# Four fused layers on one core: frequency gate's product and sum on GpSimd, layer 0's MLP finished ahead of layer 3, an order of its own for the last image's MLP rounds

## Chip, cores and metric

The kernel runs on one core of one Trainium2 chip. The metric is the device time of one execution in microseconds, the median of several executions. A core has five engines that run beside each other, each in its own program order: TensorE (PE, matmuls; its weight loads are listed as PEld), VectorE (DVE), ScalarE (ACT), GpSimd (POOL) and SyncE (SP, which here only issues DMAs). An engine that waits for a semaphore holds everything behind it in its order.

## What is computed

Four images of 192 channels and 64 x 64 pixels go through four layers; all is fp32. Layer 0 is a transformer block with a deformable 3x3 convolution for the queries, channel attention and an MLP. Layer 1 is a non-local block (4096 x 4096 scores an image). Layer 2 is attention in overlapping windows, followed by a projection, a frequency gate and a gated MLP. Layer 3 is a masked 3x3 depthwise convolution whose weights depend on the image's mean. What the change touches, cut from the reference:

```python
# layer 0, end
h1 = layer_norm(xs2, gamma2, beta2)
xs3 = xs2 + gelu(h1 @ w_fc1 + b_fc1) @ w_fc2 + b_fc2
# layer 2, after the windows
def _hft(x, w, b):
    a = 3.0 * x
    for s in (2, 4, 8):
        a = a - upsample(mean_pool(x, s), s)
    return sigmoid(dwconv3(a, w, b)) * x
x1 = x + _hft(conv1x1(out, proj_w, proj_b), hft_w, hft_b)
z = gelu(conv1x1(ln_c(x1), fc1_w, fc1_b))
z1, z2 = split(z, 2, axis=1)                      # 384 channels each
z = z1 * dwconv3(ln_c(z2, sgn_g, sgn_b), sg_w, sg_b)
return x1 + conv1x1(z, fc2_w, fc2_b)
```

A layer norm here needs 1 / sqrt(variance + eps). In parts of the kernel it is Sqrt on ACT and a reciprocal on DVE, in others Ln and Exp (with the factor -0.5) on ACT alone.

## The kernel before

The images are handled one after the other, with work of the next image woven in. For each image b:

1. `keys` (L910): the non-local block's keys and values from layer 0's result, which `mlp0` has written to DRAM in eight chunks. For b = 1 and 2, `offsets(b + 1)` (eight layer norms and the deformable convolution's offsets for the image after) goes chunk by chunk with it.
2. `layer1`: scores (L963) and their product with the values (L1031); the deformable convolution's gather for image b + 1 is woven in.
3. `windows`: layer 2's attention.
4. `rest(b)`: `project`, `mlp`, `layer3`. For images 0 to 2, the steps of `mlp0(b + 1)`, layer 0's attention result and MLP for the next image, are woven in: each part of `rest` yields a credit, and each whole credit takes one step of `mlp0`. What is left of `mlp0` when `layer3` has been issued is drained at the end (`for _ in other`). The last image (`alone`) has nothing to weave in; there some of the depthwise taps run as matmuls with diagonal weights on PE (`HFT_PE`, `GATE_PE`).

`project` handles six units of 128 x 1024. `first(u)` projects (L1475), builds the pools and the filtered image (L1482 to L1513). `second(u)` does the nine depthwise taps (helper lines L1370, L1373 and L1377, on DVE; `gt`, `ht` and L1368 are taps on PE), the sigmoid (L1523, ACT), the product with the projected image (L1525) and the sum into `x` (L1526). `ahead()` starts the layer norm of the MLP's first pair of chunks. The order of instructions on the engines is Tile's scheduler's there; roots are Sqrt (L362) and reciprocal (L364), because the list `in_order` is empty.

`mlp` has four rounds j, one for each pair of chunks, in an order written out by hand (`tc.manual_schedule`): `widen` (L1574, L1576, GELU L1580) of six blocks of 128 hidden channels; the gate's layer norm (`gate_mean` L1586, `gate_difference` L1590, `gate_square` L1595, `gate_variances`, `gate_scale` L1613 and L1617); the depthwise taps of the pair before (`upper_taps`, five of them; `lower_taps` four more one round later, ending in L1647, which makes `z1`); `narrow` (L1659 and L1664) of the pair two rounds back; `end` (L1673) adds into `x`. In it the roots are Ln and Exp, and `table()` loads the ACT table that comes next, once.

`layer3` takes the mean, makes the weights (L1771 to L1789), then for six units ACT starts (L1819), DVE adds three taps (L1838), and a DMA stores the unit (L1840, L1844).

The lines that set the handover, in `rest`:

```python
yield from project(b, x, others, oi.pop(), psums, HFT_PE if alone else (), ahead)
yield from mlp(b, x, sums, sb, psums, GATE_PE if alone else (), hn)
yield from layer3(b, x, sums, psums, alone)
...
for part in main():
    credit += part
    while credit >= 1.0:
        next(other, None)
        credit -= 1.0
for _ in other:
    pass
```

`NCH` is 8, the number of chunks of 512 pixels; `mlp0` has 33 steps.

Of the kernel before, what the change touches and what calls it, by code (L numbers as in the profile page):

```python
# [13 lines left out]
ALU = mybir.AluOpType  # L14
# [19 lines left out]
LN_EXP, GELU = "natural_log_exp_and_others", "gelu"  # L34
# [47 lines left out]
def conv_seq_kernel(ctx: ExitStack, tc: tile.TileContext, a, out: bass.AP):  # L82
# [1340 lines left out]
    def project(b, x, others, oi, ps, taps, ahead):  # L1423
# [3 lines left out]
        with ExitStack() as s:  # L1427
# [88 lines left out]
            def second(u):  # L1516
# [25 lines left out]
    def mlp(b, x, sums, sb, ps, taps, hn):  # L1542


        with ExitStack() as s:
# [134 lines left out]
            with tc.manual_schedule():  # L1680
                in_order.append(None)
                for j in range(pairs):
                    lo, hi, upper, lower = 2 * j, 2 * j + 1, j - 1, j - 2
                    if lower >= 0:
# [11 lines left out]
                    if upper >= 0:  # L1696
                        upper_taps(upper, 0, 2)
                    end()
                    widen(j, (5, 0))
                    gate_mean(lo)  # L1700
                    gate_mean(hi)
                    if upper >= 0:
                        upper_taps(upper, 0)
                        upper_taps(upper, 1, 2)
                    gate_difference(lo)
                    gate_square(lo)
                    gate_difference(hi)
                    widen(j, (1,))
                    gate_square(hi)
                    widen(j, (2,))  # L1710
                    if upper >= 0:
                        upper_taps(upper, 1)
                        upper_taps(upper, 2, 2)
                    gate_variances(lo, hi)
                    norm = None
                    if j + 1 < pairs:
# [3 lines left out]
                    if norm is not None:  # L1720
# [5 lines left out]
                    if norm is not None:  # L1726
# [3 lines left out]
                for m in range(3):  # L1730
                    lower_taps(pairs - 2, m)
                    yield 1.0
                narrow(pairs - 2, (0, 1, 2))
# [314 lines left out]
```

## Time and profile before

| what | us |
|---|---|
| median of 3 runs | 6800.64 (6798.39 to 6806.05) |
| profiled execution | 6757.88 |
| its span | 6756.1 |
| PE busy | 6155.1 |
| DVE busy | 4694.1 |
| ACT busy | 3599.2 |
| POOL busy | 2065.4 |
| projection of image 0 | 1866 to 1999 |
| its MLP | 1999 to 2303 |
| layer 3 and the handover to image 1 | 2303 to 2336 |
| keys and layer norms of image 1 | 2336 to 2456 |
| layer 1 of image 1 begins | 2456 |
| projection of the last image | 6339 to 6443 |
| its MLP | 6437 to 6722 |
| its layer 3 | 6722 to 6756 |

The profile shows one execution. Busy shares over the whole span mix stages with different limits, so the prediction reads them by stage. Lines of a group name an instruction's source line, engine, operation, and output and input tiles by the program's names. After "idle" stands the time in which the engine did nothing before such an instruction, and what ended it.

### The profile page before, as it was taken

The numbers are of one execution on the slowest core, as the hardware profiler recorded it, in microseconds if no ns is written. First come the engines' busy times: TensorE is split into PE (matmuls) and PEld (weight loads), VectorE is DVE, ScalarE is ACT, GpSimd is POOL, SyncE is SP. The second block draws the span as 40 slices with busy tenths as digits, with TensorE's granted clock in tenths as the row PEclk, the third lists the DMA queues.
The fourth block names the chain that finished last, engine by engine and source line by source line (L and its number), as shares of the span: only waits on it lengthen the run. The fifth ranks groups of instructions, "written<-read, shape, count | busy, mean of one in ns | idle before, by whom it ended". The sixth has DMA issues, their size and how long they took to land.

```text
span 6756.1 us, 115795 instructions
## 1 busy us (share of the span) xinstructions
PE 6155.1 (91%) x45392; PEld 4180.0 (62%) x45392; DVE 4694.1 (69%) x6908; ACT 3599.2 (53%) x6136; POOL 2065.4 (31%) x2276
## 2 busy tenths in 40 slices
PE   7687999999989899999998899999998889999986
PEld 4455578786644458887654457878664457776532
DVE  3664279985677758996576848988567867765656
ACT  3664368774444358885444338877444435544332
POOL 2654057662200027672210007765220000012200
PEclk8788999999989899999999999999999999999998
DMA  6885156661010156663110047665101010010000
GB/s 188 260 280 177 54 177 217 215 196 42 8 43 15 59 181 200 219 211 93 29 31 26 17 132 218 216 208 165 35 24 30 17 54 10 15 28 22 4 7 21
DMA packets 330496, 699.37 MB, mean 104 GB/s; under 512 B 60077, under 2 KB 217181, under 8 KB 329182
## 3 DMA queue, kind: packets, MB, share of 16 engines
q0 software_dynamic: 92736, 455.22, 21.0%
q1 hardware_dynamic: 236382, 235.95, 12.3%
q8 instruction: 358, 5.87, 0.4%
q14 instruction: 188, 1.54, 0.1%
q10 hardware_dynamic: 832, 0.79, 0.0%
HBM read 611.25 MB, written 78.87 MB: 102 GB/s over the span
## 4 chain that ended last, share of the span: by engine, by line
PE 51%; DVE 17%; ACT 4%; issue 4%; DMA 2%; SPq 0%; POOL 0%; another core or an unknown queue 0%; DVEq 0%; ACTq 0%; POOLq 0%
PE y L1031 8%; PE s L963 7%; PE h L634 3%; PE v L1196 2%; PE h L1574 2%; DVE ha L1377 2%; PE qk L1121 2%; PE qk L1122 2%; PE t L1204 1%; DVE gate L1377 1%; PE zm L1586 1%; DVE ga L1377 1%; PE h L1576 1%; PE s L1157 1%; PE rb L1270 1%
## 5 line engine op out<-in xcount | busy, mean ns | idle before, releaser
L616 POOL DMA_INDIRECT ring<-table,idx x1152 | 1634.7, 1419 | 1132.5 <-issue 217.8
L963 PE MATMUL s<-ths,ph 96*128 96x256 f32 x4096 | 991.5, 383 | 8.5 <-ACT xo L626 2.7
L963 PEld LDWEIGHTS s<-ths,ph 96*128 96x128 f32 x4096 | 784.0, 193 | 137.1 <-ACT ths L957 4.7
L622 ACT ACTIVATE row<-ring,pos 128x384 f32<-128x384 f32 x1152 | 672.0, 608 | 204.3 <-DVE xo L627 111.3
L1031 PE MATMUL y<-sc,gx 128*97 128x256 f32 x3008 | 724.7, 383 | 18.4 <-ACT yn L1037 15.1
L623 DVE SCALAR_TENSOR_TENSOR row<-ring,fr,row 128x384 f32<-128x384 f32 x1152 | 674.8, 613 | 91.6 <-ACT row L622 63.1
L1031 PEld LDWEIGHTS y<-sc,gx 128*97 128x97 f32 x3008 | 492.5, 165 | 150.8 <-ACT yn L1037 16.5
L626 ACT ACTIVATE xo<-row,pos 128x192 f32<-128x192 f32 x1152 | 485.8, 448 | 156.9 <-remote 63.8
L627 DVE SCALAR_TENSOR_TENSOR xo<-row,fr,xo 128x192 f32<-128x192 f32 x1152 | 447.1, 412 | 123.3 <-issue 60.6
L1028 DVE TENSOR_TENSOR sc<-sc,mbs 128x1024 f32<-128x1024 f32 x376 | 453.4, 1218 | 46.1 <-ACT mbs L989 26.5
L965 ACT COPY sc<-s 128x1024 f32<-128x1024 f32 x376 | 377.5, 1004 | 177.5 <-PE s L963 141.5
L970 DVE TENSOR_TENSOR top<-top,sc 128x1024 f32<-128x1024 f32 x282 | 344.5, 1222 | 137.4 <-ACT sc L965 115.9
L634 PE MATMUL h<-ti,xo 128*128 128x192 f32 x2304 | 437.1, 328 | 0.0
L1029 ACT ACTIVATE sc<-sc 128x1024 f32<-128x1024 f32 x376 | 393.4, 1053 | 75.6 <-DVE sc L1028 66.5
L634 PEld LDWEIGHTS h<-ti,xo 128*128 128x128 f32 x2304 | 390.9, 190 | 29.0 <-issue 8.6
L1180 DVE TENSOR_REDUCE es<-ex 128x6 f32<-128x384 f32 x264 | 133.3, 546 | 365.0 <-ACT ex L1176 365.0
L634 PE MATMUL h<-kept,xo 128*128 128x192 f32 x960 | 255.9, 402 | 114.1 <-DVE xo L627 61.5
L634 PEld LDWEIGHTS h<-kept,xo 128*128 128x128 f32 x960 | 183.0, 224 | 209.5 <-DVE xo L627 98.6
L1624 POOL COPY gate<-gate 128x192 f32<-128x192 f32 x12 | 4.2, 351 | 1000.4 <-ACT gate L1617 855.0
L1377 DVE SCALAR_TENSOR_TENSOR ga<-gate,v,ga 128x1024 f32<-128x1024 f32 x234 | 300.4, 1284 | 6.7
L1031 PE MATMUL y<-se,gx 128*97 128x256 f32 x1088 | 268.3, 387 | 8.6 <-ACT se L1029 8.1
L858 ACT ACTIVATE gl<-h,bias_fc 128x256 f32<-128x256 f32 x384 | 151.2, 474 | 232.9 <-PE h L851 232.5
(391 smaller groups left out, 11213.0 us busy)
## 6 DMA issues: line engine op xcount, KB each, us to landing
ti<-table SPq DMA_DIRECT2D x768, 48.0 KB
ring<-table,idx POOLq DMA_INDIRECT x1152
xnd<-xn SPq DMA_DIRECT2D x4, 3270.0 KB
xi<-in_x_dram SPq DMA_DIRECT2D x32, 384.0 KB
xk<-xd SPq DMA_DIRECT2D x32, 384.0 KB
xd<-xc SPq DMA_DIRECT2D x64, 192.0 KB
table<-tt SPq DMA_DIRECT2D x32, 384.0 KB
xc<-xd SPq DMA_DIRECT2D x60, 192.0 KB
```

The costliest lines, as they stand in the source:

```text
L616: nc.gpsimd.indirect_dma_start(out=gt.rearrange("p q r c -> p (q r c)"), out_offset=None, in_=corners, in_offset=bass.IndirectOffsetOnAxis ...
L622: nc.scalar.activation(row, gt[:, 0], AF.Copy, scale=pos[:, t, 9 + tap : 10 + tap])
L623: nc.vector.scalar_tensor_tensor(row, gt[:, 1], fr[:, t, 9 + tap : 10 + tap], row, ALU.mult, ALU.add)
L626: nc.scalar.activation(xo[:, j, :], row[:, 0, :], AF.Copy, scale=pos[:, t, tap : tap + 1])
L627: nc.vector.scalar_tensor_tensor(xo[:, j, :], row[:, 1, :], fr[:, t, tap : tap + 1], xo[:, j, :], ALU.mult, ALU.add)
L634: nc.tensor.matmul(acc[m // 2][:, bass.ts(m % 2, C)], lhsT=xo.rearrange("p j c -> p (j c)")[:, bass.ts(m, 128)], rhs=tt, start=t == 0 and ...
L963: nc.tensor.matmul(p[:, t, :], lhsT=ph[:, bass.ts(G * g + t, 128)], rhs=ths[i], start=True, stop=True)
L965: nc.scalar.copy(to, p)
L1028: nc.vector.tensor_tensor(ex, ex, mbs[i].unsqueeze(1).to_broadcast([128, G, QN]), ALU.add)
L1029: nc.scalar.activation(ex, ex, AF.Exp)
L1031: nc.tensor.matmul(py, lhsT=gx[:, G * g + t, :], rhs=ex[:, t, :], start=g == 0 and t == 0, stop=g == NG - 1 and t == G - 1,)
L1377: nc.vector.scalar_tensor_tensor(acc[:, b], src(tap, b), w[:, tap : tap + 1], acc[:, b], ALU.mult, ALU.add)
```

## The change

Four things are changed.

- In `project`, product and sum of the frequency gate go from VectorE to GpSimd. `project` runs with ACT's instructions in program order and `in_order` active, so that its layer norms, and those of `mlp0` that are woven in there, take their roots by Ln and Exp, and tables are loaded ahead by `table()`.
- In `mlp` for images 0 to 2, `narrow(lower, (0, 1))` and `narrow(lower, (2,))` become one `narrow(lower, (0, 1, 2))`; the tail's credits go from 0.5, 0.6 and 0.7 to 0.9 each; after `mlp` a credit of 32 lets all of `mlp0` be issued ahead of `layer3`.
- In `mlp` for the last image the round has an order of its own: the narrow comes after the second widen, means and differences; the upper taps stand later, two of the three in the norm's steps; the tail puts upper taps of the last pair between lower taps of the one before, and narrows block by block.
- The output DMAs of `layer3` go from SP's queue to GpSimd's for images 0 to 2.

The diff, cut to its core:

```diff
-            if name == GELU:
-                nc.scalar.preload_act_table(AF.Gelu)
+            if name in (GELU, SIGMOID):
+                nc.scalar.preload_act_table(name)
...
+                table(SIGMOID)
                 nc.scalar.activation(acc, acc, AF.Sigmoid, bias=VW["l2_hftb"][:, k])
                 cols = bass.ts(u, UN)
-                nc.vector.tensor_tensor(acc, acc, prs.pop(u), ALU.mult)
-                nc.vector.tensor_tensor(x[:, cols], x[:, cols], acc, ALU.add)
+                nc.gpsimd.tensor_mul(acc, acc, prs.pop(u))
+                nc.gpsimd.tensor_add(x[:, cols], x[:, cols], acc)
...
                     if lower >= 0:
                         lower_taps(lower, 2)
-                        narrow(lower, (0, 1))
-                        narrow(lower, (2,))
...
+                    if taps:
+                        widen(j, (5, 0))
+                        gate_mean(lo)
+                        gate_mean(hi)
+                        gate_difference(lo)
+                        gate_square(lo)
+                        gate_difference(hi)
+                        if lower >= 0:
+                            narrow(lower, (0, 1, 2))
+                        end()
+                        widen(j, (1,))
+                        gate_square(hi)
+                        if upper >= 0:
+                            upper_taps(upper, 0, 2)
+                        widen(j, (2,))
+                        gate_variances(lo, hi)
+                        if upper >= 0:
+                            upper_taps(upper, 0)
+                            upper_taps(upper, 1, 2)
+                    else:
+                        if lower >= 0:
+                            narrow(lower, (0, 1, 2))
...
                     yield 1.0
-                    if norm is not None:
+                    if taps and upper >= 0:
+                        upper_taps(upper, 1)
+                        upper_taps(upper, 2, 2)
+                    if more:
                         links(norm, VARIANCE)
...
+                one, two = pairs - 2, pairs - 1
+                if taps:
+                    lower_taps(one, 0)
+                    upper_taps(two, 0)
+                    lower_taps(one, 1)
+                    upper_taps(two, 1)
+                    narrow(one, (0,))
+                    lower_taps(one, 2)
+                    narrow(one, (1,))
+                    narrow(one, (2,))
+                    upper_taps(two, 2)
                     end()
-                    yield 0.5
-                    upper_taps(pairs - 1, m)
-                    yield 0.6
-                    lower_taps(pairs - 1, m)
-                    yield 0.7
-                narrow(pairs - 1, (0, 1))
-                narrow(pairs - 1, (2,))
+                    for m in range(3):
+                        lower_taps(two, m)
+                        narrow(two, (m,))
+                else:
...
+                        yield 0.9
...
+            by = nc.sync if alone else nc.gpsimd
...
-                    nc.sync.dma_start(out=flat[0:M, bass.ts(u, UN)], in_=o)
+                    by.dma_start(out=flat[0:M, bass.ts(u, UN)], in_=o)
...
-                yield from project(b, x, others, oi.pop(), psums, HFT_PE if alone else (), ahead)
+                with tc.manual_schedule(engines={mybir.EngineType.Activation}):
+                    in_order.append(None)
+                    yield from project(b, x, others, oi.pop(), psums, HFT_PE if alone else (), ahead)
+                    in_order.pop()
                 yield from mlp(b, x, sums, sb, psums, GATE_PE if alone else (), hn)
+                yield 4.0 * NCH
                 yield from layer3(b, x, sums, psums, alone)
```

More of the change, by code (lines that the diff above doesn't have):

```diff
@@ L33 @@
 NEG = -1.0e30
-LN_EXP, GELU = "natural_log_exp_and_others", "gelu"
+LN_EXP, GELU, SIGMOID = "natural_log_exp_and_others", AF.Gelu, AF.Sigmoid
 WP = 66
@@ L1683, in mlp @@
                     lo, hi, upper, lower = 2 * j, 2 * j + 1, j - 1, j - 2
+                    more = j + 1 < pairs
                     if lower >= 0:
@@ L1693, in mlp @@
                         lower_taps(lower, 2)
-                        narrow(lower, (0, 1))
-                        narrow(lower, (2,))
[L1696 to L1714, printed above, removed]
+                    if taps:
[20 more added lines that the diff above has]
+                            narrow(lower, (0, 1, 2))
+                        if upper >= 0:
+                            upper_taps(upper, 0, 2)
+                        end()
+                        widen(j, (5, 0))
+                        gate_mean(lo)
+                        gate_mean(hi)
+                        if upper >= 0:
+                            upper_taps(upper, 0)
+                            upper_taps(upper, 1, 2)
+                        gate_difference(lo)
+                        gate_square(lo)
+                        gate_difference(hi)
+                        widen(j, (1,))
+                        gate_square(hi)
+                        widen(j, (2,))
+                        if upper >= 0:
+                            upper_taps(upper, 1)
+                            upper_taps(upper, 2, 2)
+                        gate_variances(lo, hi)
@@ L1715, in mlp @@
                     norm = None
-                    if j + 1 < pairs:
+                    if more:
                         norm = pair_norm_steps(x, j + 1, sb, ps, f"l2n2_{b}_{j + 1}")
@@ L1719, in mlp @@
                     yield 1.0
-                    if norm is not None:
+                    if taps and upper >= 0:
+                        upper_taps(upper, 1)
+                        upper_taps(upper, 2, 2)
+                    if more:
                         links(norm, VARIANCE)
@@ L1725, in mlp @@
                     hns.pop(j)
-                    if norm is not None:
+                    if more:
                         hns[j + 1] = links(norm)
@@ L1729, in mlp @@
                         upper_taps(upper, 2)
[L1730 to L1733, printed above, removed]
-                for m in range(3):
-                    upper_taps(pairs - 1, m, 2)
-                    end()
-                    yield 0.5
-                    upper_taps(pairs - 1, m)
-                    yield 0.6
-                    lower_taps(pairs - 1, m)
-                    yield 0.7
-                narrow(pairs - 1, (0, 1))
-                narrow(pairs - 1, (2,))
+                one, two = pairs - 2, pairs - 1
[9 more added lines that the diff above has]
+                    upper_taps(two, 2)
+                    end()
+                    for m in range(3):
+                        lower_taps(two, m)
+                        narrow(two, (m,))
+                else:
+                    for m in range(3):
+                        lower_taps(one, m)
+                        yield 1.0
+                    narrow(one, (0, 1, 2))
+                    for m in range(3):
+                        upper_taps(two, m, 2)
+                        end()
+                        yield 0.9
+                        upper_taps(two, m)
+                        yield 0.9
+                        lower_taps(two, m)
+                        yield 0.9
+                    narrow(two, (0, 1))
+                    narrow(two, (2,))
                 end()
@@ L1843, in layer3 @@
                     for h in range(2):
-                        nc.sync.dma_start(out=to[:, :, h], in_=o[half(h)].rearrange("p (k n) -> p k n", k=2))
+                        by.dma_start(out=to[:, :, h], in_=o[half(h)].rearrange("p (k n) -> p k n", k=2))
                 yield 0.7
```

## The prediction

> **What bounds the kernel now.** I read the page's first part, then a table of stretches by stage, then the waits of TensorE (PE) inside the stretches that the change touches, then single instructions in the timeline. From the page:
>
> ```profile
> PE 6155.1 (91%) x45392; PEld 4180.0 (62%) x45392; DVE 4694.1 (69%) x6908; ACT 3599.2 (53%) x6136; POOL 2065.4 (31%) x2276
> ```
>
> PE is busy for 91% of the span, so most microseconds can only come out of PE's 600 us of idle time. The table of stretches says where it idles (columns: stretch, its length, busy us and instructions of PE, weight loads, VectorE (DVE), ScalarE (ACT), GpSimd (POOL), then granted clock, DMA share, GB/s):
>
> ```profile
> 1866.00:1999.00 133.00, 109.62 (x441) 57.50 (x440) 123.25 (x203) 55.88 (x74) 4.40 (x12) 0.87 0.16 43
> 3460.00:3591.00 131.00, 104.29 (x438) 55.08 (x437) 123.20 (x203) 55.90 (x75) 4.40 (x12) 0.90 0.15 42
> ...
> 6339.00:6443.00 104.00, 93.13 (x234) 39.11 (x234) 75.25 (x132) 26.91 (x29) 9.75 (x26) 0.91 0.05 13
> 6481.00:6531.00 50.00, 45.08 (x181) 20.70 (x181) 23.95 (x25) 20.04 (x29) 0.37 (x2) 0.93 0.00 0
> 6531.00:6600.00 69.00, 56.17 (x206) 23.93 (x206) 45.13 (x47) 20.54 (x29) 0.91 (x3) 0.90 0.00 0
> 6600.00:6656.00 56.00, 46.87 (x172) 18.80 (x170) 38.91 (x38) 14.65 (x22) 0.00 (x0) 0.97 0.00 0
> 6656.00:6722.00 66.00, 46.74 (x112) 18.14 (x112) 45.57 (x52) 6.03 (x8) 1.26 (x5) 0.87 0.02 4
> ...
> 2336.00:2456.00 120.00, 115.66 (x936) 60.96 (x935) 34.39 (x46) 40.34 (x75) 0.00 (x0) 0.93 0.48 140
> ```
>
> The first two are the projection of images 0 and 1 (image 2: 132 us, the same shares): DVE is busy 93% and PE 80 to 82%, so DVE sets the pace. The third is the last image's projection, where PE leads (90%) and DVE is at 72%. The next four are rounds 1, 2, 3 and the tail of the last image's MLP: PE idles 4.9, 12.8, 9.1 and 19.3 us, with nothing woven in. The last row is the way into layer 1 of image 1: PE is full. What PE waits for, in the projection of image 0 (columns: us in total, times, longest):
>
> ```profile
> PE pb_l0m L382 <- DVE r_l0m L364: 7.4, 2, 4.5
> ...
> PE pb_l2n L1418 <- DVE r_l2n L364: 4.5, 1, 4.5
> ```
>
> in round 2 of the last image, and in its tail:
>
> ```profile
> PE f L1659 <- DVE z L1647: 7.8, 3, 5.1
> ```
>
> ```profile
> PE f L1659 <- DVE z L1647: 18.4, 4, 12.9
> ```
>
> So two places can give time: a DVE-bound projection in which PE also waits 11.9 us for reciprocals queued on DVE, and a last MLP whose narrow matmuls stand in PE's order before work that was ready.
>
> **Part 1, the projection of images 0 to 2.** DVE loses six products (L1525, 1219 ns) and six sums (L1526, 1207 ns): 14.6 us an image; and four reciprocals (L364: 3 x 947 ns and 1753 ns), which Ln and Exp on ACT replace: 4.6 us. Together 19.2 of 123. ACT's table loads grow from 15 to 18 (1283 ns each, +3.8 us) in an engine busy 56 of 133; I take that as hidden behind DVE.
>
> GpSimd gets twelve 128x1024 operations with two inputs. The trace has none; the nearest row is L1244, 128 elements with two inputs, 0.45 us when alone. Copies give the fixed part: 528 elements 640 ns, 16 elements 195 ns, so 0.87 ns an element above 0.18 us. Lower end (two inputs at a copy's rate) 1.1 us; upper end (eight times 0.45) 3.6 us; my value (0.45 - 0.18)/128 = 2.1 ns an element, 2.3 us. Twelve take 27 us (13 to 43) of an engine that is busy 4.4 of 133. Nobody reads the sum for tens of microseconds but the pair norm, which takes units 0 and 4, two units earlier; the latency of about 6 us is covered.
>
> What is not free is the memory behind it. Two pairs in the timeline (columns: start, us, engine, line) show DVE and POOL in each other's way:
>
> ```profile
> 1681.17 0.96 DVE L1171 TENSOR_TENSOR ex<-ex,mx 128x768 f32<-128x768 f32 x1
> ...
> 1681.35 1.50 POOL L1244 TENSOR_TENSOR ot<-ot,ot 102x128 f32<-102x128 f32 x2 [15.53 <-ACT ot L1238]
> ```
>
> ```profile
> 1609.66 1.23 DVE L1171 TENSOR_TENSOR ex<-ex,mx 128x768 f32<-128x768 f32 x1
> ```
>
> The two POOL operations take 1.50 us instead of 0.90: the first ends only after the DVE operation that began before it. And the same DVE operation takes 1.23 instead of 0.96 us when a POOL copy (1609.45 to 1610.09) began first. In the projection the taps L1377, with both inputs in SBUF, are 62 of the 104 us that DVE keeps, nearly back to back. If DVE stands still for none of POOL's 27 us, it is left with 104 us and PE (110) leads; if for all of them, it has 131. My value is the taps' share, 60%: 16 us, DVE 120, 3 us less than now. For PE's waits behind reciprocals I add 2 us. **Value -5 an image, -15 in all; bounds -12 (PE's waits and its 110 us stay) and +8 (27 - 19) an image.**
>
> [...]
>
> **Part 2, the last image's projection.** DVE has room; -2 (bounds -6 and +4, by the 2.5 us that PE waits for the reciprocal and by a sum that comes late).
>
> **Part 3, rounds of images 0 to 2.** PE's order becomes 12 of L1659, then 12 of L1664. Before, 8 of L1664 (1.94 us) ran while the third z was awaited; now they stand behind that wait (0.7 us long as it was). Two rounds an image: 6 x 1.9 = +11 at most, 0 if woven work waits elsewhere anyway; value +9.
>
> **Part 4, the last image's MLP.** Round 2: after the first widen (5.7 us) PE now has widen (5.6) and means (5.4) before the narrow, so it needs z at +17, +19 and +21 us of the round; DVE's z are ready at 10.7, 15.9 and 21.1. The 7.8 us wait goes. Taps of 3.7 us each stand in the norm's chain (4.2 us waiting for the square). ACT is late next: z1 needs the buffer that the narrow reads, so its squares begin at +27, but the variances stand behind widen and taps at +36. The round ends near 57.5 instead of 68.7: -11. Round 1: only the norm's wait is filled: -3. Round 3 saves 6 to the gates' scaling. Tail: DVE no longer sits from 6678.7 to 6694 behind 60 tap matmuls (26 us); these now run in thirds of 8.7 us beside lower taps of 5.2. The last third stands behind the third narrow, so DVE waits about 10 us there. DVE's chain gives an end 10 us earlier for round 3 and tail together. **Value -24; bounds -32 and -12.**
>
> **Part 5, handover.** Layer 0's last chunk is computed before the last narrow; layer 3 comes after both. Now:
>
> ```profile
> 2325.55 8.01 PE L737 MATMUL o<-bias,ident 128*128 128x384 f32 x24 [1.36 <-DVE xa L874]
> 2335.82 1.68 PE L910 MATMUL tp<-xk,phiT 96*96 96x512 f32 x3 [2.26 <-DMA xk<-xd]
> ```
>
> The keys start some 18 us earlier (2318). But layer 3's 25 us of DVE begin near 2325 instead of 2308, and the keys' evictions stand between them in DVE's order; the fifth waits for PSUM freed near 2351. The next loads stand behind that one on SP's queue, so the third layer norm, before at 2351.7, starts near 2362. Eight norms then run one after another (76 us before), but PE is free of keys meanwhile, so the 25 us of offsets behind the last norm shrink to about 19: +3 (bounds -4 and +10), twice. From image 2 to 3 there are no norms: -3.5 (bounds -8 and +3). Output DMAs of images 0 to 2 move from SP to POOL's queue; POOL is idle there, nobody reads them.
>
> **Sum.** -15 - 2 + 9 - 24 + 6 - 3.5 = -29.5. The profiled execution has 6757.9 us (span 6756.1 and 1.8 around it), 43 us under the median 6800.64; the difference carried to the median gives **6771**.
>
> **Rivals.**
> - GpSimd is beside, not in the way: projection -12 each, in all -50, 6750. For it: L1377 beside POOL memsets keeps its 743 ns. Against: those only write.
> - GpSimd holds DVE up (the other side): operations of 3.6 us, DVE still for all 43 us, +24 an image; -14.5 + 72 = +57, 6858. It makes the kernel slower from 9.4 us an image on, that is with over 28.6 us of DVE blocked.
> - Handover: norms, not PE, set the way into layer 1, +20 each (18 us of layer 3 and 2 of queue) in place of +3: in all +4.5, 6805.
> - The last image's order gives 5 instead of 24, because DVE's taps are the chain: -10.5, 6790.
>
> **Chances.** Forecast 0.50, GpSimd free 0.15, GpSimd in the way 0.15, handover 0.12, last order 0.08. A measurement of this kernel tells 0.2% (13.6 us) from no change. Faster: 0.47 of the forecast and 0.15, 0.62; same: 0.03 + 0.09 of the handover + 0.08, 0.20; slower: 0.15 + 0.03, 0.18. Range 6742 to 6816: it leaves out most of the second rival (0.13) and the far ends of the others (0.05), and takes in the handover and the last order; the forecast's own range is 6755 to 6787.
>
> **What would show it.** The projection's stretch: 128 us, its L1526 on POOL at 2.3 us (over 3 speaks for the second rival), L1377's mean above 1275 ns or DVE idle behind POOL. Round 2 of the last image: no wait of L1660 on DVE, 57 us between its widens. The tail from the last gate to layer 3: 56 us. First L910 after image 0's MLP some 18 us earlier against the MLP's start, the first score matmul of layer 1 within 10 us. Wrong above all if DVE's taps lengthen by more than 20 us an image.

## The result and the profile after

The changed kernel takes **6901.47 us** (median of 4 runs, 6872.33 to 6915.78) against 6803.35 for the kernel before on the same chip (6798.39 to 6807.80): a ratio of 1.0145, with a 95% interval of 1.0115 to 1.0175. It is slower by 98 us; the forecast was 6771, faster by 30. The profiled execution has 6872.33 us, its span 6870.6. The experiments ran on other chips, where the kernel before takes 6622 to 6627 us and the changed kernel is slower by a ratio of 1.0123 (1.0098 to 1.0149); so ratios are compared, or times of one chip. Lines of the changed kernel stand one or two above those of before (L1525 is L1526, L1659 is L1660, L1647 is L1648).

The line of the page that opened the prediction, now:

```profile
PE 6229.8 (91%) x45392; PEld 4225.4 (62%) x45392; DVE 4687.1 (68%) x6847; ACT 3604.0 (52%) x6153; POOL 2182.2 (32%) x2348
```

PE runs the same 45,392 matmuls and is busy 75 us longer with them, and the mean granted clock went from 0.952 to 0.941: this is the first hint. The table of stretches (columns as in the prediction: stretch, length, busy us and count of PE, weight loads, DVE, ACT, POOL, then granted clock, DMA share, GB/s), for the projection of image 0, the last image's projection and its round 2, and the keys of image 1:

```profile
1886.00:2013.90 127.90, 102.94 (x418) 53.90 (x417) 114.29 (x180) 57.15 (x77) 35.03 (x22) 0.88 0.14 40
6464.00:6572.00 108.00, 88.79 (x216) 37.18 (x217) 69.33 (x115) 25.63 (x29) 32.92 (x36) 0.86 0.05 13
```

```profile
6665.30:6721.60 56.30, 51.63 (x205) 22.34 (x204) 45.13 (x46) 20.65 (x30) 0.64 (x2) 0.98 0.00 1
```

```profile
2352.00:2504.50 152.50, 137.05 (x964) 72.62 (x962) 57.65 (x84) 45.49 (x80) 8.76 (x22) 0.79 0.44 130
```

Three readings. In the projection DVE is busy 114 of 128 us although 14.6 us of products and sums and 4.6 of reciprocals are gone from it. The stretch that the prediction took for this stage, 1866 to 1999, ends 7.5 us inside the MLP; up to the MLP's first matmul the kernel before has

```profile
1866.70:1991.50 124.80, 102.25 (x420) 54.34 (x419) 116.56 (x196) 54.73 (x73) 4.40 (x12) 0.87 0.16 44
```

so DVE is busy 2 us less than before, and the stage is 4 us longer (128.7 us from its first matmul to the MLP's, against 124.8). Round 2 of the last image takes 56.3 us instead of 68.7. The keys of image 1 take 152.5 us instead of 120, at a granted clock of 0.79 instead of 0.93.

Put stage by stage (from the first instruction of a stage to that of the next), with the changed kernel's second profile, that of the control below, beside a kernel whose projections, MLPs and keys of images 0 to 2 are those of before (`e2_last_order`), both on the experiments' chips; in us, images 0, 1, 2:

| stage | unchanged | changed | difference |
|---|---|---|---|
| projection | 123.7, 123.3, 124.8 | 129.5, 129.0, 129.0 | +15.7 |
| MLP, to the next image's first key | 343.0, 343.2, 343.6 | 337.8, 338.5, 341.0 | -12.5 |
| keys, to layer 1 | 120.1, 119.7, 27.9 | 153.3, 153.1, 54.9 | +93.6 |
| last projection | 98.1 | 107.9 | +9.8 |
| last MLP and layer 3 (unchanged: profile of before) | 319.4 | 298.5 | -20.9 |

The sum is +85.7; the medians of the changed kernel's chip differ by 80.0 (6704.93 and 6624.93). Stretches that the change does not touch differ by 3 to 10 us between these two profiles (29 in all, not in the table), so a few us in one stage say little. Nearly all of the loss is the keys at the three handovers; GpSimd's part, the two rows of projections, is a quarter of that, and the last image's order gives what was forecast.

**What the keys do.** PE's timeline of the changed kernel where the keys of image 1 begin (columns: start, us, engine, line, operation, tiles, shapes, count, and in brackets the idle time ahead and what ended it):

```profile
2351.38 1.96 PE L910 MATMUL tp<-xk,phiT 96*96 96x512 f32 x4
...
2356.23 0.25 PE L1812 MATMUL pt<-mean,w1T 128*48 128x1 f32 x2
...
2357.44 1.05 PE L1823 MATMUL pw<-t,w2T 48*128 48x1 f32 x8
2358.42 0.88 PE L1826 MATMUL pw<-t,w2T 48*64 48x1 f32 x16
2359.23 2.17 PE L915 MATMUL g<-gT,xk 96*128 96x96 f32 x16
2361.20 3.62 PE L910 MATMUL tp<-xk,phiT 96*96 96x512 f32 x4
2364.61 3.57 PE L915 MATMUL g<-gT,xk 96*128 96x96 f32 x16
...
2392.62 3.73 PE L910 MATMUL tp<-xk,phiT 96*96 96x512 f32 x4 [1.84 <-DVE gx L918]
```

Four L910 take 1.96 us at the start and 3.62 from 2361 on: half clock. The granted clock is 0.5 for 58.0 us here, for 58.0 and 54.6 at the other two handovers. The kernel before has this too, but for 17.1 us at the first two and not at all at the third. Its timeline at image 2:

```profile
3926.27 2.38 PE L910 MATMUL tp<-xk,phiT 96*96 96x512 f32 x4 [2.10 <-DMA xk<-xd]
...
3931.80 3.62 PE L910 MATMUL tp<-xk,phiT 96*96 96x512 f32 x4
3935.22 3.57 PE L915 MATMUL g<-gT,xk 96*128 96x96 f32 x16
3938.58 3.62 PE L910 MATMUL tp<-xk,phiT 96*96 96x512 f32 x4
3941.99 3.25 PE L394 MATMUL pm_l<-xi,mean 96*96 96x512 f32 x4
3945.08 1.92 PE L915 MATMUL g<-gT,xk 96*128 96x96 f32 x16
3946.84 1.88 PE L910 MATMUL tp<-xk,phiT 96*96 96x512 f32 x4
```

PE is busy for 50.6 us of each of the three longer stretches and for all of the 17.1, and at a granted clock of 0.5 half of that is taken as lost (four L910 lose 1.66 of 3.62 us), so the clock alone costs (50.6 - 17.1) / 2 = 17 us, again 17, and 25 at image 3: 59 of the 93.6, as an estimate.

The traces also show behind what the half clock ended. In all sixteen of them the granted clock changes only on a grid of 3.41 us; a step is one such stretch. In the fence above it came back after the step from 3941.33 to 3944.74, the first that held nothing but matmuls of 512 columns: the end of a key's L910 and, directly behind it, L394 of the first layer norm. Of 356 steps at half clock in all traces with only L910, L915 and L394 in them, 334 were filled to less than 98% by L910 and L394, and the clock came back behind two of these; it came back behind 20 of the other 22 (in the traces before and after alone, behind none of 52 and all of 3). In the kernel before a layer norm stands behind the third L910, and there the half clock ends; in the changed kernel all norms stand behind all keys, and between them L915 with its 96 columns comes after every L910. This is read off the traces; no experiment varied it alone.

The last line of the changed kernel's fence shows the other part of the loss: a key waits for the eviction (L918) of an earlier one. DVE's timeline of the changed kernel shows where evictions stand:

```profile
2388.21 3.63 DVE L1880 SCALAR_TENSOR_TENSOR out<-x,w,out 128x448 f32<-128x448 f32 x6 [2.47 <-issue]
...
2392.02 0.55 DVE L918 COPY gx<-g 128x384 f32<-128x384 f32 x1
...
2406.53 0.56 DVE L918 COPY gx<-g 128x384 f32<-128x384 f32 x1 [6.22 <-PE g L915]
2409.94 1.22 DVE L398 TENSOR_TENSOR d_l<-xi,pm_l 96x1024 f32<-96x1024 f32 x1 [2.85 <-PE pm_l L394]
```

They stand between layer 3's taps (L1880), and the first layer norm (L398) of the image after comes behind all eight keys, 58.6 us after the first key; before, norms and keys alternated from +19.0 us on. The last of the eight norms is 119.6 us behind the first key instead of 82.6.

### The profile page after: what moved, and what is told of

Read it like the earlier page. It is cut to its first block, busy times and chain, and to the rows that moved or that the text cites. A ratio compares the mean times of both kernels' runs of the same rounds, so it can differ in the third digit from the quotient of the medians.

```text
span 6870.6 us, 115882 instructions
## 1 busy us (share of the span) xinstructions
PE 6229.8 (91%) x45392; PEld 4225.4 (62%) x45392; DVE 4687.1 (68%) x6847; ACT 3604.0 (52%) x6153; POOL 2182.2 (32%) x2348
## 5 line engine op out<-in xcount | busy, mean ns | idle before, releaser
L1377 DVE SCALAR_TENSOR_TENSOR ga<-gate,v,ga 128x1024 f32<-128x1024 f32 x234 | 300.3, 1283 | 6.5
L858 ACT ACTIVATE gl<-h,bias_fc 128x256 f32<-128x256 f32 x384 | 150.7, 474 | 237.2 <-PE h L851 236.7
```

Source lines behind the costliest of these rows:

```text
L1377: nc.vector.scalar_tensor_tensor(acc[:, b], src(tap, b), w[:, tap : tap + 1], acc[:, b], ALU.mult, ALU.add)
```

## The experiments

**1. Undo the handover** (changed kernel; everything else kept):

```diff
-                        yield 0.9
+                        yield 0.5          # and 0.6, 0.7
...
-            by = nc.sync if alone else nc.gpsimd
+            by = nc.sync
...
-                yield 4.0 * NCH
```

> The changed kernel with the handover alone undone: no credit of 32, the tail's credits 0.5, 0.6 and 0.7 again, layer 3's output DMAs on SP's queue. Theory A (the loss is in the handover: the keys of the next image run among layer 3's instructions, their evictions wait on VectorE, and the granted clock falls to 0.5): the three stretches from projection to layer 1 lose their 26 to 31 us each, so 6901 - 85 = about 6815, ratio to before about 1.002. Theory B (GpSimd's product and sum hold VectorE up, in the projection and wherever else): hardly a change, 6890 or more. Theory C (a lower clock over the whole run): no change.

Measured: 6650.86 us, ratio 1.0051 (1.0032 to 1.0071). The keys are back at 112.2, 119.4 and 27.9 us, projections stay at 127 to 129, the last MLP at 298.6. The keys of image 1 kept the clock and took 112.2 us, those of image 2 lost it for 17 us and took 119.4. Of the changed kernel's 1.2% some 0.7% go with the handover.

**2. The last image's order alone** (kernel before, with the new order of rounds and tail for the last image only).

```diff
+                    if taps:
+                        widen(j, (5, 0))
...
+                    else:
+                        if lower >= 0:
+                            narrow(lower, (0, 1))
+                            narrow(lower, (2,))
```

> The kernel before with the last image's order of rounds alone. The trace of after has this MLP at 262 us instead of 284, so theory A and B both expect 6803 - 22 = 6781, ratio 0.997; if the gain comes only from what the projection before it leaves over, it is below 10 us.

Measured: 6596.00 us, ratio 0.9968 (0.9947 to 0.9988). In the profile the last MLP takes 291.9 us instead of 319.4, a gain of 27.5; the medians show 21 to 26 (the interval reaches from 8 to 35). This part is right, in kind and in size.

**3. Product and sum back on DVE** (changed kernel, order of ACT and the roots by Ln and Exp kept):

```diff
-                nc.gpsimd.tensor_mul(acc, acc, prs.pop(u))
-                nc.gpsimd.tensor_add(x[:, cols], x[:, cols], acc)
+                nc.vector.tensor_tensor(acc, acc, prs.pop(u), ALU.mult)
+                nc.vector.tensor_tensor(x[:, cols], x[:, cols], acc, ALU.add)
```

> The changed kernel with product and sum of the frequency gate back on VectorE (ACT's order and the roots by Ln and Exp stay). Theory A: the projections were 4, 4, 1 and 10 us longer; without GpSimd's hold on VectorE's second input they give these back and perhaps the 6 us that the roots save: -20 to -40, 6860 to 6880. Theory B: most of the loss, about 6815.

Measured: 6674.40 us, ratio 1.0085 (1.0055 to 1.0116), 25 us below the changed kernel by the ratios, whose intervals overlap. The projections take 123.8, 122.2, 123.8 and 96.4 us, those of the kernel before; the roots by Ln and Exp, kept here, give nothing that can be seen. The first projection in the table of stretches:

```profile
1805.00:1928.80 123.80, 104.16 (x420) 54.62 (x418) 110.75 (x191) 57.12 (x77) 4.46 (x12) 0.88 0.17 45
```

DVE is busy 6 us less than the kernel before in a stage of the same length (116.8 of 123.7 us in `e2_last_order`): taking work off DVE did not shorten it.

**4. GpSimd alone** (kernel before, the same two lines turned round).

```diff
-                nc.vector.tensor_tensor(acc, acc, prs.pop(u), ALU.mult)
-                nc.vector.tensor_tensor(x[:, cols], x[:, cols], acc, ALU.add)
+                nc.gpsimd.tensor_mul(acc, acc, prs.pop(u))
+                nc.gpsimd.tensor_add(x[:, cols], x[:, cols], acc)
```

> The kernel before with nothing but product and sum on GpSimd (scheduler's order of ACT, Sqrt and reciprocal). Theory A (GpSimd holds VectorE: 27 us of GpSimd an image cost as much as the 14.6 us taken off VectorE, and what reads x waits): each of images 0 to 2 some 5 us longer, the last 8 to 10: 1.003 to 1.005. Rival (the loss of the projection comes from ACT's hand order and its table loads): no change or faster, at most 1.001.

Measured: 6690.95 us, ratio 1.0092 (1.0067 to 1.0117). The projections take 137.5, 137.5 and 137.9 us instead of 124. The first of them in this kernel's table of stretches:

```profile
1807.40:1945.00 137.60, 105.95 (x421) 55.86 (x420) 127.49 (x189) 55.68 (x74) 31.32 (x22) 0.86 0.14 38
```

DVE has eight instructions fewer there than before and is busy 127.5 us, where it was 116.8 in `e2_last_order`. How that comes about is seen in the changed kernel, in POOL's timeline and in DVE's beside it:

```profile
1918.52 2.72 POOL L1526 TENSOR_TENSOR ha<-ha,pr 128x1024 f32<-128x1024 f32 x1 [4.58 <-ACT ha L1524]
1921.31 3.22 POOL L1527 TENSOR_TENSOR x<-x,ha 128x1024 f32<-128x1024 f32 x1
```

```profile
1917.73 4.59 DVE L1377 SCALAR_TENSOR_TENSOR ha<-hft,wide,ha 128x1024 f32<-128x1024 f32 x2
1922.24 2.84 DVE L1490 TENSOR_TENSOR pt<-pr 128x512 f32<-128x512 f32 x1
1925.01 1.27 DVE L1377 SCALAR_TENSOR_TENSOR ha<-hft,wide,ha 128x1024 f32<-128x1024 f32 x1
```

Two taps last 4.59 us where one alone takes 1.27, and the L1490 behind them 2.84 where its mean was 0.69. The product on POOL ends at 1921.24, and the second tap at 1922.32, 1.08 us later; the sum on POOL ends at 1924.53, and L1490 at 1925.08, 0.55 us later, each time less than the instruction's own length. So each of the two stands still until the POOL operation that had begun before it is over. The other way round, POOL is held up too: the sum takes 3.22 us because the tap runs in its first microsecond, and the product's longest is 6.2 us, beside taps of 128x512 that DVE runs back to back in 0.74 us each, as before (columns of this row: shortest, median, longest in ns).

```profile
L1526 POOL TENSOR_TENSOR ha<-ha,pr x24: 2337/2359/6185, 1918.5 to 6579.3; 128x1024 f32<-128x1024 f32 x24
```

Instructions with PSUM as an input were not stretched: in the changed kernel L874 began nine times under a POOL operation and took 0.75 us at 128x512 and 0.48 at 128x256, as before. L1373, with one input in SBUF, took 0.98 us instead of 0.75 where it began under a POOL operation, so a hold on a second input alone is not what the trace shows. The 13.7 us an image are near what the prediction's own terms give for a DVE that stands still for all of POOL's time: 27 less the 14.6 us taken off it, +12.4; its +8 also took off the 4.6 us of reciprocals, which stay on DVE here. PE's wait of L844 for DVE grows beside it, from 3.8 us in `e2_last_order` to 8.4.

The rest of this experiment's loss is not GpSimd's. The keys of image 3 take 53.4 us instead of 27.9; experiment 7 shows why.

**5. Evictions on ACT** (changed kernel, so that no eviction stands behind layer 3's taps):

```diff
-            nc.vector.tensor_copy(gx[:, bass.ts(i, 4), 0:P], p)
+            nc.scalar.copy(gx[:, bass.ts(i, 4), 0:P], p)
```

> The changed kernel with the keys' second eviction (L918) on ScalarE instead of VectorE, where layer 3's taps stand. Theory A: the small waits of TensorE go, the granted clock comes back to 1.0 in the keys (0.50 in after), each handover is 15 to 25 us shorter: 6901 - 60 = about 6840. Rival within A (the loads on SP's queue and the norms placed behind all keys set the handover): less than 15 us in all, clock still near 0.5.

Measured: 6680.47 us, ratio 1.0102 (1.0064 to 1.0140): at most a small gain on 1.0123. PE's wait for gx is gone from the keys of all three images, yet they take 159.2, 149.1 and 32.3 us. At images 1 and 2 the half clock lasts 64.8 and 54.6 us; at image 3 it ends after four matmuls, and there the keys are short. The wait for the eviction was not what kept the keys long.

With four buffers for the keys' inputs in addition, so that loads wait for nothing:

```diff
-                    b, ph, gx, s2.enter_context(pool_of(name="l1k", bufs=2 if 0 < b < B - 1 else 4)),
+                    b, ph, gx, s2.enter_context(pool_of(name="l1k", bufs=4)),
```

> Run e4 (evictions on ScalarE) with four buffers for the keys' loads in the middle images too. In e4 the keys of image 3, which have four, came from 55 us to 32 at a clock of 1.0, those of images 1 and 2, which have two, stayed at 0.5. Theory A (waits of 1 to 2 us in the keys keep the clock at 0.5): the keys of images 1 and 2 take 30 us instead of 55, and the stretch to layer 1 gets 15 to 25 us shorter each: ratio 1.004 to 1.006. Rival (the layer norms of the image after, which stand behind all keys in TensorE's order, set the end): keys shorter, but the norms' chain of 66 us begins only 20 us earlier if it waits for the keys alone and not earlier if it waits for layer 3's buffers: then no gain, 1.010.

Measured: 6701.13 us, ratio 1.0135 (1.0098 to 1.0172). No gain: keys of 143.2, 151.1 and 50.6 us, half clock for 31, 65 and 48 us. The number of buffers was not the cause either.

**6. The control** (the changed kernel again, beside the experiments).

> The changed kernel itself, as the control on this chip for the others of this call. Both theories: ratio to before 1.0115 to 1.0175, as measured.

Measured: 6704.93 us, ratio 1.0123 (1.0098 to 1.0149). Its stages stand in the table above.

**7. Merged narrow undone as well** (kernel of experiment 1):

```diff
-                            narrow(lower, (0, 1, 2))
+                            narrow(lower, (0, 1))
+                            narrow(lower, (2,))
```

> Run e1 (handover undone) with the narrow of images 0 to 2 split again, so that what is left of the change is the projection and the last image's order. If the merged narrow costs the 10 us by which e1's MLPs of images 0 to 2 were longer than those of e2 (353 against 343): ratio 1.000, 30 us under e1. If those 10 us come from GpSimd's late sums: as e1, 1.005.

Measured: 6650.29 us, ratio 1.0036 (1.0012 to 1.0059). The MLPs are shorter by 5.6, 7.4 and 6.7 us than in experiment 1, 20 in all, and the median is the same. The profile shows where a like amount went: the keys of image 3 take 51.2 us instead of 27.9, those of image 1 120.0 instead of 112.2. What differs at their start, by some tenths of a microsecond, is the pause between the filler matmuls (L737) and the first key. Three kernels, PE's timeline; first `e2_last_order`:

```profile
5375.67 7.26 PE L737 MATMUL o<-bias,ident 128*128 128x384 f32 x22
5384.79 1.96 PE L910 MATMUL tp<-xk,phiT 96*96 96x512 f32 x4 [1.86 <-DMA xk<-xd]
```

then this experiment:

```profile
5389.54 2.19 PE L910 MATMUL tp<-xk,phiT 96*96 96x512 f32 x4 [2.10 <-DMA xk<-xd]
5391.52 3.57 PE L915 MATMUL g<-gT,xk 96*128 96x96 f32 x16
```

and GpSimd alone (`e6_gpsimd_alone`):

```profile
5433.99 2.83 PE L910 MATMUL tp<-xk,phiT 96*96 96x512 f32 x4 [2.33 <-DMA xk<-xd]
5436.61 3.57 PE L915 MATMUL g<-gT,xk 96*128 96x96 f32 x16
```

After a pause of 1.86 us the keys run at full clock; after 2.10 and 2.33 they fall to half clock within the first key, for 48 and 61 us. The pause is the time that a load still needs when the filler is over. Its length alone does not decide: `e2_last_order` lost the clock ahead of image 1's keys after 1.81 us. What separates the cases is how much of the pause falls into one of the clock's steps of 3.41 us. From `e2_last_order`, the steps in which the keys of images 1 and 3 begin, each with the next (columns of the table of stretches; clock third from the end):

```profile
2267.07:2270.48 3.41, 1.65 (x4) 0.76 (x5) 0.38 (x2) 0.00 (x0) 0.00 (x0) 1.00 0.95 268
2270.48:2273.89 3.41, 3.41 (x16) 3.13 (x15) 0.00 (x0) 0.68 (x1) 0.00 (x0) 0.50 0.18 60
...
5383.44:5386.85 3.41, 2.06 (x7) 1.02 (x8) 0.00 (x0) 0.07 (x1) 0.00 (x0) 1.00 0.99 247
5386.86:5390.27 3.41, 3.41 (x22) 2.37 (x21) 0.56 (x1) 0.62 (x2) 0.00 (x0) 1.00 0.97 235
```

PE stands still for 1.76 us of the first and for 1.35 us of the third. Of the fifteen handovers with a pause (kernel before, experiments 1, 2, 4 and 7), the eleven with 1.76 to 2.34 us of it in the step lost the clock, and the four with 1.25 to 1.46 us kept it.

**8. More filler at the handover** (kernel of experiment 2; 16 matmuls in place of 12 in the filler ahead of the keys):

```diff
             if i == NCH - 1:
-                keep_warm(p[:, 0:384], 12)
+                keep_warm(p[:, 0:384], 16)
```

> The kernel before with the last image's order and 16 instead of 12 filler matmuls ahead of the keys (nothing reads their results), so that TensorE does not stand still for the 1.9 to 2.3 us until the keys' first load lands. Theory A (a pause of about 2 us ahead of the keys costs the clock, which then stays at 0.5 for 17 us in images 1 and 2 and, in some executions, for all the keys of image 3): keys of images 1 and 2 start at a clock of 1.0, 120 us become 112; 6603 - 20 in the median, ratio 0.993 to 0.995. Rival (the clock falls for another reason): as run e2, 0.997, or slower by the 2.7 us of filler each.

Measured: **6583.21 us, ratio 0.9949 (0.9930 to 0.9968)**, the fastest kernel of this study, below both kernels of the comparison. The pause is gone (0.2 us are left at image 1) and with it the half clock (table of stretches, keys of image 1; the clock is the third number from the end):

```profile
2268.40:2381.00 112.60, 107.85 (x936) 56.56 (x936) 34.42 (x46) 40.33 (x75) 0.00 (x0) 1.00 0.52 149
```

112 us instead of 120, twice: that is the 17 us of half clock of the kernel before, halved. The medians of this kernel and of experiment 2 were taken beside different runs, and their intervals overlap; the gain over experiment 2 rests on the profile.

**9. Roots by Ln and Exp on top of it** (kernel of experiment 8, product and sum on DVE):

```diff
+                table(SIGMOID)
                 nc.scalar.activation(acc, acc, AF.Sigmoid, bias=VW["l2_hftb"][:, k])
...
-                yield from project(b, x, others, oi.pop(), psums, HFT_PE if alone else (), ahead)
+                with tc.manual_schedule(engines={mybir.EngineType.Activation}):
+                    in_order.append(None)
+                    yield from project(b, x, others, oi.pop(), psums, HFT_PE if alone else (), ahead)
+                    in_order.pop()
```

> Run e9 with ACT's order by hand and the roots by Ln and Exp in the projection, product and sum on VectorE. In e3 the projections with these roots took 123.3 us in the mean, those of e2 123.9: no difference to e9 beyond 0.2%, though the prediction gave the roots 4.6 us of VectorE and 2 us of TensorE's waits in each of three images, which would be 0.997 of e9.

Measured: 6593.87 us, ratio 0.9954 (0.9937 to 0.9972). Against experiment 8 the projections of images 0 to 2 are 2 to 3 us shorter and the MLPs 2 to 5 us longer: no gain.

**10. Filler inside layer 3** (changed kernel; 12 filler matmuls behind layer 3's last one-column matmul, images 0 to 2):

```diff
+            if not alone:
+                keep_warm(ps.tile([128, CN], F32, tag="h", name=f"warm3_{b}")[:, 0:384], 12)
```

> The changed kernel with 12 filler matmuls (6 us at full clock, nothing reads them) behind layer 3's one-column matmuls of images 0 to 2, which in this kernel stand among the keys. Theory A (the clock is lost at those matmuls and does not come back in the keys): the clock comes back, keys of image 3 take 32 to 40 us instead of 55, the stretch of images 1 and 2 about 140 instead of 153; 6705 - 30 to - 45, ratio 1.005 to 1.008. Rival (waits on VectorE's evictions set the pace of the keys and the clock only follows): the fillers add their 6 us each, 1.014 or more.

Measured: 6694.21 us, ratio 1.0113 (1.0094 to 1.0131). PE's timeline at image 3:

```profile
5441.86 0.88 PE L1826 MATMUL pw<-t,w2T 48*64 48x1 f32 x16
5442.68 8.01 PE L737 MATMUL warm<-bias,ident 128*128 128x384 f32 x24
...
5452.28 1.88 PE L910 MATMUL tp<-xk,phiT 96*96 96x512 f32 x4
...
5467.92 3.73 PE L910 MATMUL tp<-xk,phiT 96*96 96x512 f32 x4 [7.02 <-DVE gx L918]
```

The filler's 12 matmuls are listed as 24. Behind them the clock is still full, where it fell at this place in the changed kernel; the keys then run ahead of DVE, wait 7.0 us for an eviction behind layer 3's taps, and now the clock is lost (four L910 take 3.73 us). The three handovers take 150.7, 149.8 and 60.3 us, 8 us of filler in each, where 6 had been expected. Both parts of the loss are in these lines: each stands behind the other, so that removing one gives little.

**11. Layer 3's taps left out** (changed kernel, images 0 to 2):

```diff
-                    for to, up in rows:
+                    for to, up in rows if alone else ():
```

> The changed kernel with layer 3's three taps on VectorE left out for images 0 to 2 (25 us of VectorE each are not done, so those images are not layer 3's result). Theory A': VectorE's order sets the keys, since the evictions stand between layer 3's taps: without the taps the keys of image 3 take 28 to 35 us, those of images 1 and 2 some 30, and the stretch of images 1 and 2 is 130 to 140 us (the norms still stand behind the keys): 6705 - 50 to - 75. Rival (the clock alone: lost at layer 3's one-column matmuls, whatever VectorE does): the keys of image 3 stay at 50 us or more with no wait in them, less than 25 us in all.

Measured: 6690.58 us, ratio 1.0083 (1.0053 to 1.0113). Without any tap in DVE's way the keys still take 143.1, 142.9 and 50.2 us. PE's timeline at image 3:

```profile
5446.02 3.43 PE L910 MATMUL tp<-xk,phiT 96*96 96x512 f32 x4
5449.25 3.57 PE L915 MATMUL g<-gT,xk 96*128 96x96 f32 x16
...
5486.47 1.91 PE L955 MATMUL th<-xc,thetaT 96*96 96x256 f32 x4
```

No matmul waits until layer 1 (L955), and the six pairs of L910 and L915 from 5446.02 to 5486.47 take 6.7 us each instead of the 3.5 of the kernel before. The clock is the main part. The keys are 10, 10 and 5 us shorter than with the taps, but the half clock is shorter too: PE is busy in it for 37.6, 41.0 and 47.2 us instead of 50.6, and half of the difference is 7, 5 and 2 us. That leaves 3 to 5 us a handover for the taps themselves.

**12. The order of the keys by hand** (changed kernel; PE and SP in written order for norms and keys of images 1 and 2, so that they alternate as before):

```diff
-                    for _ in range(NCH):
-                        next(parts)
-                        next(making, None)
+                    with tc.manual_schedule(engines={mybir.EngineType.PE, mybir.EngineType.SP}):
+                        for _ in range(NCH):
+                            next(parts)
+                            next(making, None)
```

> The changed kernel with TensorE's and SP's instructions of keys and layer norms of images 1 and 2 in the order of the program, one norm and one chunk of keys in turn, as the order was before by the scheduler's choice. If it is the norms standing behind all keys that makes the stretch 153 us: back to some 125 to 135, 6705 - 40 = 6665, ratio 1.006. If layer 3 on VectorE sets it: VectorE still does layer 3 first, both norms and keys wait 26 us for it, no gain or a loss, 1.011 to 1.016.

Measured: 6753.25 us, ratio 1.0191 (1.0170 to 1.0213), the slowest. The keys' first matmul now comes behind layer 3: the MLP's stage takes 383 us instead of 338, with one wait of 28 us of PE for a norm's square on ACT. The keys take 136.6 and 119.1 us. ACT's timeline has what that square stood behind:

```profile
2282.75 2.50 ACT L1861 ACTIVATE out<-x,wide,w 128x1008 f32<-128x1008 f32 x2 [10.72 <-DMA out_dram<-out]
...
2302.52 1.06 ACT L401 ACTIVATE sq_l<-d_l 96x1024 f32<-96x1024 f32 x1 [15.38 <-DMA out_dram<-out]
```

Layer 3's starts (L1861) wait for buffers that its output DMAs free, the square behind them in ACT's order goes only once such a DMA has landed, and PE, now in written order, holds all keys behind it. Without that DMA it would have gained 5 us at most: the square's input (L398) comes from DVE at 2297.73, behind all of layer 3's taps. Alternating by hand does not mend it; that the scheduler put the keys first because the norms could not go is a guess.

**13. The early drain undone** (changed kernel; credits of 0.9 and output DMAs on POOL's queue kept):

```diff
-                yield 4.0 * NCH
```

> The changed kernel without the credit of 32 alone (the tail's credits stay at 0.9, the output DMAs on GpSimd's queue). If it is this line that makes the handover slow, as run e1: ratio 1.005 and a stretch of 120 us in images 1 and 2. If the credits or the queue do it: as the changed kernel, 1.012.

Measured: 6711.17 us, ratio 1.0126 (1.0100 to 1.0152), the same as the changed kernel, with keys of 156.4, 153.3 and 50.7 us. So the line that looks like the handover is not what makes it: the credits of the tail, or the queue, do. This was not what I had thought of that line; credits and queue were not taken apart.

## Why the prediction was wrong

**Part 1, projection: -15 forecast, +16 measured.** The POOL operation was sized right (2.3 us forecast, 2.36 median), and in the changed kernel so was its hold on DVE: against experiment 3 some 12 us of products and sums are gone from the stretch and DVE is busy 114.7 us instead of 110.7, so it was held for 16 us, the figure forecast. No run shows that the taps alone are held, so that this was "the taps' share" is luck: L1490 and L1493 are held like the taps (L1490's mean went from 686 to 1418 ns, that of L1493 at 128x256 from 422 to 929), and in experiment 4 the same working gives 23 of POOL's 27 us. The step that failed is "so DVE sets the pace", by which the stage was to be as long as DVE is busy, with ACT "hidden behind DVE" and 2 us less of PE's waits. DVE's busy time fell by 2 us (forecast 3), but its idle time in the stage went from 6.9 to 14.8 us (`e2_last_order` and control), and the stage grew by 6 (5 in the mean of three); experiment 3 shows the same without GpSimd: less work, more idle time, no shorter. Waits between PE, ACT and DVE fill what is taken off DVE: PE's waits for the reciprocals on DVE are gone, and others have come (projection of image 0; columns: us, times, longest):

```profile
PE pp L1478 <- ACT pr L1482: 6.0, 1, 6.0
PE o L870 <- ACT gl L858: 5.7, 1, 5.7
```

The sign named for it beforehand did show: L1377's mean rose above 1275 ns, to 1427. The row's own bound, DVE still for all of POOL's time, was +8 an image; 5 were measured, and 13.7 with the roots left on DVE. That was the better end for the time.

**Part 2, last projection: -2 forecast, +10 measured.** Its bound of +4 came from a late sum. The cost is at another place: the tap matmuls (L1368) wait for the filtered image, which DVE makes behind stretched instructions; 6.3 us before, now

```profile
PE ht L1368 <- DVE x L1513: 13.1, 1, 13.1
```

That is 7 of the 10 us.

**Part 3, merged narrow: +9 forecast, about +20 measured** (experiments 1 and 7, one profile each). Its bound of 11 counted the eight matmuls that no longer fill the wait for z; the difference is 6.6 us an image instead of 3.8 at most. What fills the rest was not followed.

**Part 4, last MLP: -24 forecast, -21 measured in the changed kernel and -27.5 alone.** Right by its own steps: round 2 in 56.3 us (57.5 forecast), and there PE waits 1.1 us for z instead of 7.8. The wait for z in the tail that was forecast at about 10 us is there; in round 3 and tail it is

```profile
PE f L1660 <- DVE z L1648: 11.6, 5, 8.2
```

**Part 5, handovers: +2.5 forecast, some +61 measured** (MLP and keys together +81, less part 3). The step that failed is "PE is free of keys meanwhile, so the 25 us of offsets behind the last norm shrink to about 19". Three things were taken wrongly:

- The clock. The sum took keys at full clock. They ran at half for 55 to 58 us at each handover: 59 us of loss by the estimate above. This is the largest term, and the sum put it at nothing; no rival had it. The rows were there to read: the prediction's own fence shows three L910 in 1.68 us at the start of the keys of image 1 and a granted clock of 0.93 in that stretch, and the timeline shown above has 17 us of half clock behind it. A change that makes something else stand at this place puts at stake a clock that the kernel before lost at two handovers, with pauses of 2.17 and 2.01 us in a step of 3.41, and kept at the third, with 1.29.
- The norms. The third was forecast 11 us later. In fact all keys came ahead of all norms, because nothing but the scheduler orders them (experiment 12 shows what an order by hand runs into), and the last norm came 37 us later against the first key. With no norm between the keys, nothing there ended the half clock either. That the norms run at the pace of DVE, ACT and PE in turn was right; they take 61 us from first to last in the changed kernel, 64 before.
- The start of the keys. It came 5.2, 4.7 and 2.6 us earlier instead of 18; part 3's 6.6 us stand against it, which leaves 9 to 12 for the earlier end of layer 0's MLP.

The rival "handover, +20 each" had the right place and the wrong reason, and too small a price; "GpSimd holds DVE up" had part of the reason at a smaller price (+5 instead of +24 an image). They came together, and together lie beyond the range.

**What stays open.** The reading of the clock's steps comes from the traces and was not tested by an experiment made for it. In the changed kernel the half clock begins just behind layer 3's one-column matmuls (L1812, L1823, L1826), and with filler behind these it does not begin there (experiment 10), which points to them: in all traces, the 22 steps at full clock with 1.2 to 1.8 us of one-column matmuls, the keys' matmuls in the rest and no pause lost the clock (three of them in the changed kernel, with 1.7 to 1.8 us), and three of experiment 10 with filler in the rest kept it. Whether these matmuls alone do it was not tested. Some 35 of the 93.6 us lie beyond the estimate for the clock; how they divide among the norms' later place, waits for evictions and loads was not taken apart.

## What to carry to other kernels

Before an instruction is moved into or ahead of a stretch, compare the durations of the same matmul shape along that stretch: here four L910 took 1.96 us in some places and 3.62 in others, and the clock was the largest part of the price. Behind a pause of 2.0 to 2.2 us the kernel before stood at half clock for 17 us, behind 1.7 to 1.8 us of one-column matmuls the changed kernel for 55 to 58; by the estimate above that is 17 to 25 us more a handover, and the work that was moved off VectorE is 14.6 us an image. Look also at what brings the clock back: here it was an unbroken run of 512-column matmuls (behind 20 of 22 such steps), which the new order took away. An engine that is busy for 93% of a stage need not set its length: 6 us less work on VectorE made the projection 0 to 3 us shorter, and the whole no faster (experiments 3 and 9). Moving 14.6 us of element-wise work an image from a VectorE at 93% to GpSimd freed VectorE of less than it seemed: its own instructions with two SBUF inputs (L1377, L1490, L1493) waited for GpSimd's, in the first projection for some 16 us. And undo each part of a change alone: here the part that was right was worth 0.3% and was hidden under two that were not; with four more filler matmuls it makes 0.5%.

## What the runs showed of the hardware

- The granted clock changed only on a grid of 3.41 us, between 1.0 and 0.5 (traces before and after). At the fifteen handovers with a pause ahead of the keys it fell to 0.5 where PE stood still for 1.76 us or more of a step (kernel before: 2.17 and 2.01) and stayed full at 1.46 us or less (kernel before: 1.29); by length alone, a pause of 1.81 us lost it and one of 1.86 us did not (`e2_last_order`).
- Once lost among fp32 matmuls of 96x512 and 96x96, it stayed at half for 17 (kernel before) to 48 us (`e7_narrow_split`) without a gap in PE's work, and for 61 with 0.6 us of gaps (`e6_gpsimd_alone`). It came back behind 20 of 22 steps filled to 98% or more by the 512-column ones and behind 2 of 334 others.
- In the changed kernel a 128x1024 fp32 product on GpSimd took 2.34 us at the least and 2.36 in the median, and up to 6.2 beside VectorE taps back to back; one 128x1024 tap with two SBUF inputs took 1.27 us alone, and two took 4.59 us beside it.
